# Graph attention layer on one core: where three table merges stand on the vector engine, and the order of the layer norm's steps

## The chip, the cores and the metric

The kernel runs on one core of one Trainium2 chip. The metric is the device time of one execution in microseconds (us). The engines are named as in the profile: PE (TensorE matmul, with its weight loads PEld), DVE (VectorE), ACT (ScalarE), POOL (GpSimd) and SP (SyncE, which issues most DMAs). Each engine works through its own queue in order.

## The reference

`x` is 384 x 1024 (nodes by features). The layer normalises it, projects it to q, k and v, projects each a second time, and runs attention with 16 heads of 64 under a mask built from a list of 6528 typed edges:

```python
h = jnp.maximum(_layernorm(x, axis=-1), 0.0)
q = h @ wq.T + bq;  k = h @ wk.T + bk;  v = h @ wv.T + bv
q2 = (q @ wiq.T + biq).reshape(N, H, D).transpose(1, 0, 2)   # k2, v2 alike
w = jax.nn.softplus(edge_type_weights)
mask = jnp.full((N, N), -jnp.inf).at[src, dst].set(w[edge_type - 1])
mask = mask.at[idx, idx].set(jnp.where(jnp.isneginf(diag), w[3], diag))
scores = jnp.einsum('hnd,hmd->hnm', q2, k2) * scale + mask[None]
out = jnp.einsum('hnm,hmd->hnd', softmax(scores), v2)
return x + (out.transpose(1, 0, 2).reshape(N, OUT_F) @ wo.T + bo)
```

## The kernel before, in words

**Number format.** Matrices are split into a rounded high part and a low part (the remainder). A product is then three matmuls: high x high, high x low and low x high (`mm3`, L367 to L369). Each weight chunk of 128 x 1024 is loaded by SP into `raw` (L65), its high part is made on ACT (`split_hi`, L77) and its low part on DVE or POOL (`split_lo`, L82).

**Layer norm (first part of the span).** The nodes are three tiles of 128. For each tile DVE computes mean and variance (`ln_bn` L251, `ln_mean` L254, with the negated mean on ACT in L257), the mean is subtracted in two halves (`ln_sub`: tiles 0 and 1 on ACT, L280, and POOL, L282; tile 2 on DVE, L284), PE transposes the eight 128 x 128 blocks into two PSUM banks (`ln_transpose`, L292), ACT takes the ReLU as the high part (`ln_hi`, L298) and DVE the low part (`ln_lo`, L303). Division by the standard deviation is postponed: `ln_root` (L260) and `ln_rstd` (L264 to L268) give 1/std per node, `ln_row` (L274, L275) turns it into a row `rrow`, and each projection's result is multiplied by that row (L382, then L383 and L384). `warm(n)` puts n transposes of the identity on PE whose results nobody reads (L309). PE's first real work is the product of weight 0 with the tiles (L414), then weight 1 (L367 to L369).

**Softplus of the edge weights.** `softplus_a` (L157, L158) is on DVE; `softplus_b` (L161, L162, L164: exp, ln, and a small exp) is on ACT and needs it; `softplus_c` (L167, L168) is on DVE again; `mask_values` (L172 to L175) on POOL uses the result.

**The mask.** DVE looks for edges that occur twice (L217), POOL scatters the values into three tables in DRAM (L228), and near the end of the k projections the tables are loaded back (`mask_load`, L237). `mask_select(g)` merges table g into the mask `ma`: one predicated copy of 128 x 1152 on DVE (L241). The first score needs all three.

**Groups of q2 and k2.** Weight chunks 32 to 47 are q2 and k2 of head pairs 0 to 7 in turn: 32 is q2 of pair 0, 33 is k2 of pair 0, 34 is q2 of pair 1, and so on. A group is 24 matmuls into one PSUM bank. Before group w is put on PE, `qk_head(w)` issues the work beside it: `pendq.pop(0)()` is `qk_done` of the group before, which evacuates its bank into `nat` (L377 on ACT, L378 on DVE) and issues the DMAs that stack the parts into `qs` and `ks` (L557 to L567). `split_hi(w + 2)`, `split_lo(w + 2)` and `load(w + 4)` prepare later weights. For the first three groups the order of these steps is a different one (`first`).

**Attention.** One loop goes over 48 steps (16 heads x 3 tiles). It is written out by hand: the scores of step i (`do_S`, L692, two PSUM banks in turn), the softmax steps of earlier i (L698 on DVE reads the scores and adds `ma`; L702 exp on ACT; L706 and L707 normalise), the transposes (L712) and the products with v2 (L729). Between them `fill` puts matmuls of the q2/k2 groups, and later of the output projection. The first 84 units of `fill` (groups 32, 33, 34 and half of 35) come ahead of the first score. The order on each engine is the order of the program; no scheduler changes it.

Of the kernel before, what the change touches and what calls it, by code (L numbers as in the profile page):

```python
# [11 lines left out]
AF = mybir.ActivationFunctionType  # L12
OP = mybir.AluOpType
# [5 lines left out]
EPS = 1e-5  # L19
# [3 lines left out]
def gnn_kernel(ctx: ExitStack, tc: tile.TileContext, x, edges, erows, etw, wq, wk, wv, wiq, wik, wiv, wo,  # L23
# [6 lines left out]
    nc = tc.nc  # L30
# [8 lines left out]
    EB = 8  # L39
    NTAB, RNG = 3, EC // 3  # L40
    JI = [0, 1, 3, 5, 8, 11, 14, RNG]
    WARM = (20, 6, 4)

    def bank(tag):
        return psum.tile([128, 512], F32, tag=tag, name=tag, bufs={"g": 3, "a": 1}.get(tag, 2))
# [14 lines left out]
    def load(w):  # L60
        if w >= NCH:
            return
        n, m = chunks[w]
        raw[w] = wpool.tile([128, D], F32, tag="raw", name="raw", bufs=3)
        nc.sync.dma_start(raw[w], W[n][m])  # L65

    def split_hi(w, dst=None, dve=False):
        if w >= NCH:
            return
        if dst is None:  # L70
            t = wpool.tile([128, 2, D], F32R, tag="whl", name="whl", bufs=4)
            dst = (t[:, 0, :], t[:, 1, :])
        whl[w] = dst
        if dve:
            nc.vector.tensor_copy(dst[0], raw[w])
        else:
            nc.scalar.activation(dst[0], raw[w], AF.Copy)  # L77

    def split_lo(w, eng=None):
        if w < NCH:  # L80
            hi, lo = whl[w]
            (eng or nc.vector).tensor_tensor(lo, raw[w], hi.bitcast(F32), OP.subtract)  # L82

    def split(w, lo_eng=None, dst=None, hi_dve=False):
        split_hi(w, dst, hi_dve)
        split_lo(w, lo_eng)
# [24 lines left out]
    epsc = const.tile([128, 1], F32, name="epsc")  # L111
# [18 lines left out]
    def mask_consts():  # L130
        nc.gpsimd.memset(upper, 1.0)
        nc.gpsimd.affine_select(upper, upper, pattern=[[1, 128]], compare_op=OP.is_gt, fill=0.0, base=0,
                                channel_multiplier=-1)
        nc.gpsimd.iota(dump.bitcast(I32), pattern=[[0, 1]], base=CELLS, channel_multiplier=1)
        nc.gpsimd.tensor_copy(w8[:, 8:9], dump.bitcast(I32))
        nc.gpsimd.memset(zero, 0.0)
# [12 lines left out]
    def mask_floats():  # L149
        nc.gpsimd.tensor_copy(ed.bitcast(F32), ed)  # L150
# [5 lines left out]
    def softplus_a():  # L156
        nc.vector.tensor_scalar(w8[:, 0:4], ew, 0.0, None, op0=OP.max)  # L157
        nc.vector.scalar_tensor_tensor(w8[:, 4:8], ew, -1.0, ew, op0=OP.mult, op1=OP.min)  # L158
# [21 lines left out]
    def key_rows():  # L180

        nc.gpsimd.tensor_copy(kf, er)
        nc.gpsimd.tensor_scalar(kf[:, :EC], kf[:, :EC], float(N), None, op0=OP.mult)
        nc.gpsimd.tensor_tensor(krt[:, :EC], kf[:, :EC], kf[:, EC:], OP.add)
        nc.sync.dma_start(krow.rearrange("c j -> (c j)").rearrange("(p e) -> p e", p=128), krt[:, :EC])
# [53 lines left out]
    def mask_select(g):  # L239

        nc.vector.copy_predicated(ma, mbt[g].bitcast(I32), mbt[g])  # L241
# [4 lines left out]
    var, negm, root, vq, inv, rstd = (lnt[:, c:c + NT] for c in (4, 8, 12, 16, 20, 24))  # L246
    var = lnt[:, 1:2 * NT:2]
    rrow = work.tile([128, 2, N], F32R, tag="qs", name="rrow").bitcast(F32)[:, 0, :]

    def ln_bn(t, h):  # L250
        nc.vector.bn_stats(lnt[:, 30 + 12 * t + 6 * h:36 + 12 * t + 6 * h], xt[t][:, h * 512:(h + 1) * 512])  # L251

    def ln_mean(t):
        nc.vector.bn_aggr(lnt[:, 2 * t:2 * t + 2],  # L254
                          lnt[:, 30 + 12 * t:42 + 12 * t].rearrange("p (a b) -> p a b", a=2))
        if t < 2:
            nc.scalar.mul(negm[:, t:t + 1], lnt[:, 2 * t:2 * t + 1], -1.0)  # L257

    def ln_root():
        nc.scalar.activation(root, var, AF.Sqrt, bias=epsc, scale=0.25)  # L260

    def ln_rstd():

        nc.vector.tensor_scalar(vq, var, 0.25, EPS / 4, op0=OP.mult, op1=OP.add)  # L264
        nc.vector.reciprocal(inv, root)
        nc.vector.tensor_tensor(inv, inv, vq, OP.mult)
        nc.vector.tensor_tensor(root, root, inv, OP.add)
        nc.vector.reciprocal(rstd, root)  # L268
# [8 lines left out]
    def ln_sub(t, c0, c1, eng):  # L277
        src, dst = xt[t][:, c0:c1], xn[t][:, c0:c1]
        if eng is nc.scalar:
            nc.scalar.activation(dst, src, AF.Identity, bias=negm[:, t:t + 1])  # L280
        elif eng is nc.gpsimd:
            nc.gpsimd.tensor_tensor(dst, src, lnt[:, 2 * t:2 * t + 1].to_broadcast([128, c1 - c0]), OP.subtract)  # L282
        else:
            nc.vector.tensor_scalar(dst, src, lnt[:, 2 * t:2 * t + 1], None, op0=OP.subtract)  # L284

    def ln_transpose(t):
        pss = []
        for half in range(2):
            ps = bank("st"[half] if t < 2 else "ga"[half])
            for j in range(4):  # L290
                k = half * 4 + j
                nc.tensor.transpose(ps[:, j * 128:(j + 1) * 128], xn[t][:, k * 128:(k + 1) * 128], ident)  # L292
            pss.append(ps)
        return pss

    def ln_hi(t, half, ps):
        hi = hT[:, 0, half * 4:half * 4 + 4, t * 128:(t + 1) * 128]
        nc.scalar.activation(hi, ps.rearrange("p (k n) -> p k n", k=4), AF.Relu)  # L298

    def ln_lo(t, half, ps):  # L300
        hi = hT[:, 0, half * 4:half * 4 + 4, t * 128:(t + 1) * 128]
        lo = hT[:, 1, half * 4:half * 4 + 4, t * 128:(t + 1) * 128]
        nc.vector.scalar_tensor_tensor(lo, ps.rearrange("p (k n) -> p k n", k=4), 0.0, hi.bitcast(F32),  # L303
                                       op0=OP.max, op1=OP.subtract)

    def warm(n):
        for i in range(n):
            ps = bank("g")
            nc.tensor.transpose(ps[:, :128], ident, ident)  # L309

    mask_consts()
    warm(WARM[0])
    key_rows()
# [5 lines left out]
    ln_mean(0)  # L319
    ln_sub(0, 0, 512, nc.scalar)  # L320
    ln_sub(0, 512, D, nc.gpsimd)
    ln_bn(1, 0)
    ln_bn(1, 1)
    ln_mean(1)
    p0 = ln_transpose(0)
    warm(WARM[1])
    ln_hi(0, 0, p0[0])
    ln_sub(1, 0, 512, nc.scalar)
    ln_sub(1, 512, D, nc.gpsimd)
    ln_bn(2, 0)  # L330
    ln_bn(2, 1)
    ln_mean(2)
    ln_hi(0, 1, p0[1])
    ln_sub(2, 0, 512, nc.vector)
    ln_sub(2, 512, D, nc.vector)
    p1 = ln_transpose(1)
    warm(WARM[2])
    ln_hi(1, 0, p1[0])
# [9 lines left out]
    ln_hi(2, 0, p2[0])  # L348
    ln_hi(2, 1, p2[1])
    ln_root()  # L350
    ln_lo(0, 0, p0[0])
    ln_lo(1, 0, p1[0])
    ln_lo(2, 0, p2[0])
    softplus_a()
    ln_lo(0, 1, p0[1])
    ln_lo(1, 1, p1[1])
    ln_lo(2, 1, p2[1])
    ln_rstd()
    mask_floats()
    split(1, nc.gpsimd)  # L360
    split_hi(2)
# [24 lines left out]
    w = 0  # L386
# [189 lines left out]
    def qk_head(w):  # L576
        first = w - W0 < 3
        if not first:
            load(w + 4)
            split_hi(w + 2)  # L580
        if pendq:
            pendq.pop(0)()
        if first:
            split_hi(w + 2)
        split_lo(w + 2, nc.gpsimd if (w + 2) % 2 == PAR else None)
        if first:
            load(w + 4)
        if 0 < w - W0 <= NTAB:
            mask_select(w - W0 - 1)

    def fill_qk():
        nonlocal w
        for p in range(8):
            for n in ("iq", "ik"):
                tasks.append(lambda w=w: qk_head(w))
                if now[0] < 0:
                    run_tasks()
                gps[w] = bank("g")
                src = qT if n == "iq" else kT
                for k in range(KT):  # L600
                    colmm(gps[w], w, src, k)
                    yield 3
                pendq.append(lambda w=w: qk_done(w))
                w += 1
        tasks.append(lambda: pendq.pop(0)())

    pendq = []
    W0 = 32
# [245 lines left out]
```

## Time and profile before

| what | value |
|---|---|
| median of 3 runs | 305.87 us (305.39 to 306.45) |
| the profiled execution | 305.25 us |
| its span (first to last instruction) | 303.5 us |
| PE busy | 293.2 us, 97% of the span |
| PE clock granted, mean | 0.999 |
| DVE, ACT, POOL busy | 202.3, 154.6, 156.5 us |
| the three merges, L241 | 1.54, 3.75 and 1.44 us, from 151.8, 161.0 and 165.1 us |
| the scores of steps 0, 1, 2 on PE, L692 | from 161.83, 163.22 and 167.35 us |
| first matmul of weight 0, L414 | from 13.22 us |

The span is what the trace covers; the execution's own time is 1.75 us longer. All durations below come from the one profiled execution. A line number such as L241 is a line of the kernel before; a group of instructions is named by line, engine, operation and the tiles that it writes and reads. "us" in a timeline counts from the start of the span.

### The profile page before, as it was taken

The page shows a single profiled execution, that of the slowest core. Times are in us where ns is not written, and L with a number is a line of the kernel's source. Part 1 is how long each engine was busy: PE and PEld are TensorE (multiplying, and loading weights), DVE is VectorE, ACT ScalarE, POOL GpSimd, SP SyncE. Part 2 cuts the span into 40 slices and gives each one's busy share as a digit, 9 for nine tenths or more (in the row PEclk, how much of TensorE's full clock was granted, in tenths as well). Part 3 has the DMA queues.
Part 4 walks back from the last instruction along what each step waited for, and adds up shares of the span by engine and source line. Part 5 has one row for each costly group of instructions (what it writes and reads, how often), then busy time and mean ns, then how long its engine had stood idle before and what let it go on. Part 6 is the DMA issues. An engine that isn't in the chain of part 4 may idle for free.

```text
span 303.5 us, 4966 instructions
## 1 busy us (share of the span) xinstructions
PE 293.2 (97%) x1653; PEld 276.7 (91%) x1653; DVE 202.3 (67%) x493; ACT 154.6 (51%) x288; POOL 156.5 (52%) x164
## 2 busy tenths in 40 slices
PE   6799999999999999999997999999999999999995
PEld 5699999999988889999997999999999998888884
DVE  2968976667756653888629766667675766696523
ACT  3784643334422222555224667767677766676310
POOL 4776676273766785600033547383837466557210
PEclk9999999999999999999999999999999999999999
DMA  7799845645396749393277998556665636910005
GB/s 226 284 293 379 281 148 182 223 144 176 106 311 182 231 147 287 109 350 121 90 183 208 216 209 175 150 150 163 153 171 133 176 108 158 375 57 0 2 0 207
DMA packets 22377, 55.12 MB, mean 182 GB/s; under 512 B 4816, under 2 KB 8400, under 8 KB 22352
## 3 DMA queue, kind: packets, MB, share of 16 engines
q1 hardware_dynamic: 19968, 52.42, 57.0%
q0 software_dynamic: 2064, 1.80, 2.1%
q10 hardware_dynamic: 320, 0.59, 0.9%
q8 instruction: 13, 0.21, 0.3%
q14 instruction: 12, 0.10, 0.1%
HBM read 40.39 MB, written 4.97 MB: 149 GB/s over the span
## 4 chain that ended last, share of the span: by engine, by line
PE 91%; issue 2%; DMA 2%; DVE 2%; ACT 1%; ACTq 1%; SPq 0%; DVEq 0%
PE g L367 20%; PE g L369 20%; PE g L368 20%; PE s L692 6%; PE a L729 6%; PE t L712 5%; DMA g<-in_x_dram 2%; PE s L368 2%; PE s L369 2%; PE s L367 2%; PE t L369 2%; PE t L368 2%; PE t L367 2%; PE g L414 1%; ACTq L567 1%
## 5 line engine op out<-in xcount | busy, mean ns | idle before, releaser
L367 PE MATMUL g<-g,whl 128*128 128x384 f32 x312 | 106.4, 341 | 0.0
L369 PE MATMUL g<-g,whl 128*128 128x384 f32 x312 | 104.5, 335 | 0.0
L368 PE MATMUL g<-g,whl 128*128 128x384 f32 x312 | 104.2, 334 | 0.0
L228 POOL DMA_INDIRECT tab<-val,idx x51 | 57.8, 1133 | 37.4 <-DMA tab<-val,idx 10.8
L77 ACT ACTIVATE whl<-raw 128x1024 fp32r<-128x1024 f32 x51 | 53.4, 1051 | 31.6 <-PE g L369 21.1
L707 POOL TENSOR_TENSOR e<-e,s 128x384 f32<-128x384 f32 x48 | 39.1, 828 | 43.1 <-DVE s L706 34.7
L82 DVE TENSOR_TENSOR whl<-raw,whl 128x1024 fp32r<-128x1024 f32 x41 | 50.2, 1224 | 15.5 <-ACT whl L77 15.5
L368 PEld LDWEIGHTS g<-g,whl 128*128 128x128 f32 x312 | 58.7, 188 | 0.0
L367 PEld LDWEIGHTS g<-g,whl 128*128 128x128 f32 x312 | 58.6, 188 | 0.0
L369 PEld LDWEIGHTS g<-g,whl 128*128 128x128 f32 x312 | 58.5, 188 | 0.0
L82 POOL TENSOR_TENSOR whl<-raw,whl 128x1024 fp32r<-128x1024 f32 x11 | 26.5, 2410 | 37.7 <-ACT whl L77 33.9
L383 ACT ACTIVATE g<-f,bc 128x384 fp32r<-128x384 f32 x24 | 14.8, 618 | 54.5 <-DVE f L382 54.5
L702 ACT ACTIVATE e<-e,s 128x384 f32<-128x384 f32 x48 | 29.4, 612 | 14.7 <-DVE s L698 14.7
L722 DVE TENSOR_TENSOR pt<-t,pt 128x384 fp32r<-128x384 f32 x48 | 26.4, 550 | 14.3 <-ACT pt L721 13.6
L721 ACT ACTIVATE pt<-t 128x384 fp32r<-128x384 f32 x48 | 23.3, 484 | 13.6 <-PE t L712 12.7
L692 PE MATMUL s<-ks,qs 128*128 128x384 f32 x96 | 25.3, 344 | 2.3 <-DVE s L698 2.3
L698 DVE CUSTOM_DVE_ANT_0 e<-s,ma 128x384 f32<-128x384 f32 x48 | 26.3, 550 | 0.9 <-PE s L692 0.5
L382 DVE TENSOR_TENSOR f<-g,rrow 128x384 f32<-128x384 f32 x24 | 13.3, 556 | 15.3 <-PE g L369 15.3
L712 PE MATMUL t<-ident,e 128*128 128x128 f32 x144 | 23.5, 271 | 0.0
L712 PEld LDWEIGHTS t<-ident,e 128*128 128x128 f32 x144 | 18.7, 140 | 3.1
L692 PEld LDWEIGHTS s<-ks,qs 128*128 128x128 f32 x96 | 17.1, 188 | 4.9 <-DVE s L698 4.2
L729 PE MATMUL a<-pt,vhl 128*128 128x384 f32 x96 | 20.8, 351 | 0.0
(147 smaller groups left out, 410.8 us busy)
## 6 DMA issues: line engine op xcount, KB each, us to landing
ks<-nat SPq DMA_DIRECT2D x30, 192.0 KB, 3.5
raw<-in_wv_dram SPq DMA_DIRECT2D x8, 512.0 KB, 5.9
raw<-in_wq_dram SPq DMA_DIRECT2D x8, 512.0 KB, 3.4
raw<-in_wiv_dram SPq DMA_DIRECT2D x8, 512.0 KB, 3.9
raw<-in_wk_dram SPq DMA_DIRECT2D x8, 512.0 KB, 4.6
raw<-in_wiq_dram SPq DMA_DIRECT2D x8, 512.0 KB, 3.7
raw<-in_wik_dram SPq DMA_DIRECT2D x8, 512.0 KB, 4.6
raw<-in_wo_dram SPq DMA_DIRECT2D x8, 512.0 KB, 5.0
```

Source lines behind the costliest of these rows:

```text
L77: nc.scalar.activation(dst[0], raw[w], AF.Copy)
L82: (eng or nc.vector).tensor_tensor(lo, raw[w], hi.bitcast(F32), OP.subtract)
L228: nc.gpsimd.indirect_dma_start(out=tabs[c // RNG], out_offset=bass.IndirectOffsetOnAxis(ap=idx[:, c:c + 1], axis=0), in_=val[:, c:c + 1], ...
L367: nc.tensor.matmul(ps, lhi, rhi, start=first, stop=False)
L368: nc.tensor.matmul(ps, lhi, rlo, start=False, stop=False)
L369: nc.tensor.matmul(ps, llo, rhi, start=False, stop=last)
L692: nc.tensor.matmul(ps[:, :N], qs[:, o, t * 128:(t + 1) * 128], ks[:, o, s, :], start=(s == 0), stop=(s == 1))
L702: nc.scalar.activation(es[i], es[i], AF.Exp, bias=s[:, 0:1], scale=-1.0, accum_out=s[:, 1:2])
L707: nc.gpsimd.tensor_tensor(es[i], es[i], s[:, 2:3].to_broadcast([128, N]), OP.mult)
L712: nc.tensor.transpose(ps[:, k * 128:(k + 1) * 128], es[i][:, k * 128:(k + 1) * 128], ident)
L722: nc.vector.tensor_tensor(lo, pv, hi.bitcast(F32), OP.subtract)
L729: nc.tensor.matmul(ps[:, :N], vhl[:, k, p, 2 * o:2 * o + 2, :], pts[h][:, s, k, :], start=(k == 0 and s == 0), stop=(k == 2 and s == 1))
```

## The change

Merges. The three calls of `mask_select` stand elsewhere: merge 0 at the end of the head of group 32 (before: of 33); merge 1 in the head of group 33, right behind the evacuation of group 32 (before: at the end of the head of 34); merge 2 in the head of group 34, right behind the evacuation of group 33 (before: at the end of the head of 35).

Layer norm. Both ReLUs of tile 0, with the transposes and the 6 filler transposes ahead of them, are issued ahead of the mean of tile 1. The 4 filler transposes between tiles 1 and 2 are gone. The quantity `vq` is computed on ACT behind the square root instead of on DVE in `ln_rstd`. `softplus_a` stands behind `ln_rstd`, that is behind all low parts.

On the engines' queues this is all that differs: no DMA is added, removed or reordered, and POOL's and SP's queues are the same.

```diff
-    WARM = (20, 6, 4)
+    WARM = (20, 6, 0)
...
     def ln_root():
         nc.scalar.activation(root, var, AF.Sqrt, bias=epsc, scale=0.25)
+        nc.scalar.activation(vq, var, AF.Identity, bias=epsc, scale=0.25)
 
     def ln_rstd():
 
-        nc.vector.tensor_scalar(vq, var, 0.25, EPS / 4, op0=OP.mult, op1=OP.add)
         nc.vector.reciprocal(inv, root)
...
     ln_sub(0, 512, D, nc.gpsimd)
+    p0 = ln_transpose(0)
+    warm(WARM[1])
+    ln_hi(0, 0, p0[0])
+    ln_hi(0, 1, p0[1])
     ln_bn(1, 0)
     ln_bn(1, 1)
     ln_mean(1)
-    p0 = ln_transpose(0)
-    warm(WARM[1])
-    ln_hi(0, 0, p0[0])
     ln_sub(1, 0, 512, nc.scalar)
     ln_sub(1, 512, D, nc.gpsimd)
     ln_bn(2, 0)
     ln_bn(2, 1)
     ln_mean(2)
-    ln_hi(0, 1, p0[1])
     ln_sub(2, 0, 512, nc.vector)
...
     ln_lo(2, 0, p2[0])
-    softplus_a()
     ln_lo(0, 1, p0[1])
     ln_lo(1, 1, p1[1])
     ln_lo(2, 1, p2[1])
     ln_rstd()
+    softplus_a()
     mask_floats()
...
         if pendq:
             pendq.pop(0)()
+        if 0 < w - W0 < NTAB:
+            mask_select(w - W0)
         if first:
             split_hi(w + 2)
         split_lo(w + 2, nc.gpsimd if (w + 2) % 2 == PAR else None)
         if first:
             load(w + 4)
-        if 0 < w - W0 <= NTAB:
-            mask_select(w - W0 - 1)
+        if w == W0:
+            mask_select(0)
```

## The prediction

> **What bounds the kernel now.** First the engine row of the page and busy time by stage (columns: stretch, its length, busy us and instructions of PE, PE weight load, DVE, ACT, POOL, granted clock, DMA share, GB/s):
> ```profile
> PE 293.2 (97%) x1653; PEld 276.7 (91%) x1653; DVE 202.3 (67%) x493; ACT 154.6 (51%) x288; POOL 156.5 (52%) x164
> 0.00:18.00 18.00, 13.52 (x81) 12.11 (x82) 11.68 (x26) 10.76 (x18) 12.09 (x24) 1.00 0.76 254
> 18.00:82.00 64.00, 64.00 (x369) 63.65 (x369) 47.29 (x130) 28.09 (x38) 37.71 (x38) 1.00 0.65 217
> 150.00:168.00 18.00, 15.93 (x93) 15.61 (x91) 10.70 (x11) 6.90 (x10) 4.89 (x2) 1.00 0.65 174
> 168.00:262.00 94.00, 94.00 (x568) 90.68 (x568) 62.81 (x189) 67.55 (x159) 55.48 (x53) 1.00 0.68 173
> ```
> TensorE is full between 18 and 150 us and between 168 and 262 us. It has slack only in the layer norm (first 18 us), around 150-168 us, and at the end. So the change can gain only where it closes a TensorE gap, and both its parts sit at one. The waits of PE name them:
> ```profile
> PE s L292 <- ACT g L280: 2.7, 2, 1.7
> PE s L692 <- DVE s L698: 2.3, 2, 2.1
> PE g L414 <- ACT g L298: 0.3, 1, 0.3
> ```
> Second gap: the chain of waits (start us, length us, piece), 159-168 us:
> ```profile
> 159.84 0.04 DVE whl L82
> ...
> 160.99 0.31 DVE ma L241
> 161.30 3.33 issue
> 164.62 0.61 DVE nat L378
> 165.24 1.36 DVE ma L241
> ...
> 166.73 0.15 DVE e L698
> ...
> 167.35 0.62 PE s L692 x2
> ```
> S product 2 (L692) needs the bank that S product 0 gives up at its first read, L698. DVE runs in order, and two table merges (L241), the second and third, stand before that L698. The DVE and POOL timelines give the reason why the second merge is long:
> ```profile
> 160.84 2.50 POOL L82 TENSOR_TENSOR whl<-raw,whl 128x1024 fp32r<-128x1024 f32 x1 [4.19 <-ACT whl L77]
> 160.99 3.75 DVE L241 COPY_PREDICATED ma<-mbs 128x1152 f32<-128x1152 int32 x1
> ```
> POOL ends at 163.34, and 163.34 + 1.44 (the merge of 165.14 took that) is 164.78 against a real end of 164.74. The merge stood still until POOL was done.
>
> First gap: the chain through the layer norm:
> ```profile
> 9.18 0.58 ACT g L298
> 9.76 0.62 ACT g L280
> 10.37 0.04 issue
> 10.42 0.66 PE s L292 x4
> 11.07 0.44 PE t L292 x4
> 11.51 0.49 PE g L309 x4
> 12.01 0.45 PE g L292 x4
> ```
> The ReLU of tile 0 (L298) stands ahead of the subtraction of tile 1 (L280) on ACT, though its input was ready at about 7.6; and four filler transposes (L309) sit between tiles 1 and 2.
>
> [...] The trace agrees: the merge above, and L264 (128x3), which took 1.26 us and ended at 17.21 when POOL's L82 ended (17.19). [...] The trace shows no fall: the longest PE gap here is 1.73 us and the granted clock is 1.00.
>
> **Part A, layer norm.** No DMA moves. Removed: 4 filler transposes on PE and L264 on DVE. Added: one ACT Identity of 128x3; its nearest row is L260, 0.30 us, holding ACT for 0.19 (L260 starts 13.45, the next 13.64). It is in front of the hi split of weight 1.
> 1. ACT. The two ReLUs of tile 0 run when their transposes end (about 7.6 and 8.0), and end near 8.7, before the mean of tile 1 is there (9.03): free. L280 of tile 1 needs its negated mean (L257, 9.07 to 9.27), so it starts at 9.31 as in tile 0 (0.24 after L257) and ends at 10.03, not 10.36. Transposes of tile 1 start at 10.09 against 10.42.
> 2. PE. The second half is loaded by 10.94 (0.85 after, as before; POOL's half, L282, is there at 10.15). Without the filler, tile 2's first half needs only DVE's L284 (first one ends 11.00): about 11.1. Its second half waits for the second L284, 11.75, so it starts at 11.82 and ends at 12.42.
> 3. ACT's ReLU of tile 2: first half starts about 11.76 (0.49 behind the last of tile 1), second at 12.45 against 12.97 before. L414 starts 0.14 after the first of them ends (12.35): 12.5 against 13.22. Its fifth product needs the second ReLU (13.05 + 0.14 = 13.19) and is due at 12.5 + 4 x 0.172 = 13.19. Gain **0.7 us**.
> 4. What is late next: the third product of weight 1 needs POOL's L82. ACT now reaches weight 1 at about 13.31, POOL runs 14.45 to 16.86, and PE wants it at 12.5 + 24 x 0.172 + 0.35 = 16.97. It just fits; I take **0.65**, bounds 0.3 and 0.75. Before, this had 0.5 us to spare, so POOL is the next limit.
> 5. L264 gone: I credit nothing. L266, a DVE product of two SBUF operands, now meets the same POOL L82[...]. The end of L268 moves from 17.89 to about 17.5; PE wants it at 18.7.
> 6. Softplus behind it: its two DVE instructions (0.45 and 0.15[...]) leave the ReLU low parts, which gain 0.45, but Exp on ACT now waits for about 17.9 instead of starting at 16.96. Queued behind it on ACT: two table loads (1.28 each), hi split 3, the row factor L275; behind that on DVE, lo split 3 and the first L382; on POOL, the values (L172). All come about 1 us later. Who waits: weight 3 starts on PE at about 25.5 and needs L382 done (23.3 before, now about 24.0), and the table merges are 125 us away. Cost zero; the cover is 1.5 us.
> 7. Four filler transposes are on the chain for 0.49 us; that is contained in step 2.
>
> **Part B, merges.** Same three instructions, one place earlier each; no DMA moves. They go past these: merge 0 from behind nat of group 32 (q2 of pair 0; groups 33, 34, 35 are k2 0, q2 1, k2 1) to ahead of it; merge 1 from behind lo split 36 to behind nat 32; merge 2 from behind nat 34 to behind nat 33. The DMAs of nat (L557 to L567, on SP and ACT) wait for those L378.
> 1. Merge 0: lo split 34 ends at 149.9, so it runs 149.83 to 151.3; nat 32's L378 was at 151.25. Its qs DMAs slip 0 to 0.1 us; S product 0, which needs the last ks DMA, is set by nat 33. Zero. The tables were issued by 129.84 and landed within 7.1 us, so before 137: no wait.
> 2. Merge 1 takes the place of merge 0: 151.9 to 153.4, POOL idle. Zero.
> 3. Merge 2: behind nat 33, at 155.9, while POOL's L82 runs 154.25 to 156.65: blocked, ends about 158.1. DVE's next work, lo split 36, waits for ACT until 159.84. Zero, with 1.7 us to spare.
> 4. DVE at 161: nat 34 follows ACT (161.22) at 161.25 instead of 164.62, and the first L698 follows S 0 at about 162.4 instead of 166.73. S 2 no longer waits.
> 5. What is late next: the second L698 still stands behind nat 35 and lo split 38. ACT's nat 35 is at 164.81, behind a hi split that waited for a weight load until 163.84; neither moves. So nat 35 165.4, lo split 165.95, second L698 167.1 to 167.65; S 3 at 167.7.
> 6. Sum: from 165.12, where PE stopped, S 2, nine products, S 3 and six products take 0.35 + 1.56 + 0.35 + 1.04 = 3.30, so S 4 was due at 168.42. It came at 171.17: 2.75 lost. After: S 3 due 167.03, comes 167.7: 0.67 lost. Gain **2.1 us**, bounds 1.2 (step 5 a us later, or POOL giving way to merge 2) and 2.75.
> From there PE is full for 94 us and everything is paced by it; the transfers of pair 1 are issued 1.9 us earlier too.
>
> **Sum.** 0.65 + 2.1 = 2.75 us. The profiled execution is 305.25 us (span 303.5 and 1.75 around it): 302.5. The median of the runs, 305.87, is 0.62 above it: **303.1 us**.
>
> **Rivals.**
> - *A new wait takes most of one part* (0.2): S 3 waits a us longer, or weight 1's POOL split eats A. For it: steps A4 and B5 have next to no slack. Against: both were worked out from times that the change leaves alone. Gain 1.3 to 2.0: 303.9 to 304.6.
> - *The gain is given back, or the change does not do what it says* (0.06): PE's later stages wait for DMA. Against: PE is 94.00 of 94 busy, and the pair's DMAs move along. 305.5.
> - *Slower* (0.04): without the four fillers PE's activity from 7 to 13 us falls and the clock drops to half. Half clock costs half of its duration, so it outweighs 2.75 from 5.5 us on[...]: 306.5. Against: the longest gap shrinks from 1.73 to about 1.4 us.
> - *Forecast* (0.7): 303.1, with 302.5 to 303.8 from the bounds and the spread of runs before (305.39 to 306.45).
>
> Range 302.3 to 304.6: it leaves out the two small cases and a little at either edge. A run can tell about 0.3% (0.9 us) from no change: faster 0.9, same 0.06, slower 0.04.
>
> **What would show it.** Right: L414 starts near 12.5; no L241 between 160 and 168, merge 2 over 2 us long around 156; the PE wait for L698 falls from 2.3 to under 1 us and moves to S 3; L266 ends with POOL's L82. Wrong: a PE wait for L82 on POOL near 17 us or for L698 of 2 us, a granted clock under 0.9 in the first 20 us, or a new PE wait in 25-150 us.

## The result, and the profile after

The changed kernel took 302.31 us (median of 6 runs, 301.78 to 302.95), the kernel before 305.63 us in the 6 runs beside it; the ratio is 0.989, 95% interval 0.9863 to 0.9917. Forecast were 303.1 us and 302.3 to 304.6: the sign and the order of size were right, the time lies at the lower end of the range, 0.8 us under the forecast. Against the 305.87 us that the forecast started from, 3.56 us are gone, not 2.75. The two places of the change give about 2.6 of them; where the rest comes from is the main question of the runs below.

The profiled execution took 302.19 us, its span is 300.5 us (303.5 before). Engine row of the page, and busy time by stage (the second stretch is moved 2.7 us against the one shown of before, since all comes earlier; columns as there):

```profile
PE 293.1 (98%) x1649; PEld 276.1 (92%) x1649; DVE 200.5 (67%) x492; ACT 154.9 (52%) x289; POOL 155.7 (52%) x164
0.00:18.00 18.00, 14.46 (x83) 12.55 (x84) 12.11 (x25) 11.05 (x19) 12.15 (x24) 1.00 0.83 254
147.30:165.30 18.00, 18.00 (x106) 18.00 (x105) 11.48 (x13) 7.21 (x11) 4.89 (x2) 1.00 0.70 182
```

PE does the same work (293.1 us), but in the 18 us around the first scores it is now full, where it did 15.93 before; in the first 18 us it does 0.94 us more. The waits of PE:

```profile
PE s L292 <- ACT g L280: 2.0, 2, 1.2
PE s L694 <- DVE s L700: 0.2, 1, 0.2
```

(L694 and L700 are L692 and L698 of before, two lines on.) The wait of 2.3 us for the first read of the scores is down to 0.2, and that of L414 for the ReLU is gone. The merges in the DVE timeline, with the POOL instruction beside the third:

```profile
148.86 1.55 DVE L241 COPY_PREDICATED ma<-mbs 128x1152 f32<-128x1152 int32 x1
150.29 0.61 DVE L378 SCALAR_TENSOR_TENSOR nat<-g,bc,nat 128x384 fp32r<-128x384 f32 x1
150.81 1.55 DVE L241 COPY_PREDICATED ma<-mbs 128x1152 f32<-128x1152 int32 x1
...
154.92 2.43 DVE L241 COPY_PREDICATED ma<-mbs 128x1152 f32<-128x1152 int32 x1
158.71 1.23 DVE L82 TENSOR_TENSOR whl<-raw,whl 128x1024 fp32r<-128x1024 f32 x1 [1.37 <-ACT whl L77]
...
161.39 0.56 DVE L700 CUSTOM_DVE_ANT_0 e<-s,ma 128x384 f32<-128x384 f32 x1 [0.65 <-PE s L694]
```

```profile
153.54 2.40 POOL L82 TENSOR_TENSOR whl<-raw,whl 128x1024 fp32r<-128x1024 f32 x1 [23.13 <-ACT whl L77]
```

The third merge still stands behind POOL (153.54 + 2.40 + 1.44 = 157.38; it ended at 157.35; 1.44 us is what the third merge of before took beside no POOL instruction), but now DVE has nothing to do until 158.71. At 161.39 the first read (L700) waited for the scores, and no longer the scores for the read. The chain through the layer norm:

```profile
7.16 1.30 DVE lnt L251 x2
8.48 0.22 DVE lnt L254
...
8.96 0.73 ACT g L280
9.69 0.04 issue
9.73 0.66 PE s L292 x4
10.39 0.45 PE t L292 x4
10.84 0.01 issue
10.85 0.63 PE g L292 x4
...
11.51 0.66 PE a L292 x4
12.17 0.09 issue
12.26 1.81 PE g L414 x9
```

No ReLU and no filler is on it. But note its start: L251 of tile 1 starts at 7.16 us here and at 7.50 before, because that tile of `x` landed 0.34 us earlier in this execution, which is no work of the change. Counted from there, L414 comes after 5.10 us and not 5.72: 0.62 us gained.

### The profile page after: what moved, and what is told of

It reads as the page before. It is cut to its first block, busy times and chain, and to the rows that moved or that the text cites. A ratio compares the mean times of both kernels' runs of the same rounds, so it can differ in the third digit from the quotient of the medians.

```text
span 300.5 us, 4961 instructions
## 1 busy us (share of the span) xinstructions
PE 293.1 (98%) x1649; PEld 276.1 (92%) x1649; DVE 200.5 (67%) x492; ACT 154.9 (52%) x289; POOL 155.7 (52%) x164
## 4 chain that ended last, share of the span: by engine, by line
PE 95%; DMA 2%; DVE 1%; ACT 0%; issue 0%; SPq 0%
PE g L369 21%; PE g L367 21%; PE g L368 21%; PE s L694 6%; PE a L731 6%; PE t L714 5%; PE s L369 2%; PE s L368 2%; PE s L367 2%; DMA g<-in_x_dram 2%; PE t L369 2%; PE t L367 2%; PE t L368 2%; PE g L414 1%; PE a L369 1%; PE a L367 1%
## 5 line engine op out<-in xcount | busy, mean ns | idle before, releaser
L82 DVE TENSOR_TENSOR whl<-raw,whl 128x1024 fp32r<-128x1024 f32 x41 | 50.2, 1224 | 9.6 <-ACT whl L77 7.9
L82 POOL TENSOR_TENSOR whl<-raw,whl 128x1024 fp32r<-128x1024 f32 x11 | 26.5, 2412 | 35.6 <-ACT whl L77 31.8
L700 DVE CUSTOM_DVE_ANT_0 e<-s,ma 128x384 f32<-128x384 f32 x48 | 26.3, 550 | 2.0 <-PE s L694 1.8
L694 PE MATMUL s<-ks,qs 128*128 128x384 f32 x96 | 25.3, 344 | 0.3 <-DVE s L700 0.2
L378 DVE SCALAR_TENSOR_TENSOR nat<-g,bc,nat 128x384 fp32r<-128x384 f32 x16 | 9.9, 618 | 16.4 <-ACT nat L377 14.4
```

Source lines behind the costliest of these rows:

```text
L694: nc.tensor.matmul(ps[:, :N], qs[:, o, t * 128:(t + 1) * 128], ks[:, o, s, :], start=(s == 0), stop=(s == 1))
```

## The experiments

Each ratio is to the kernel before, run beside it. Two things scatter from run to run: the landing of tile 1 of `x` (its L251 starts at 6.65 to 8.17 us in the profiles), and the granted clock that the records of each run show. In most runs its mean is 0.997 to 1.000, in others about 0.994, in some 0.988. Over all sets of runs beside the experiments the kernel before had 64 of 111 at 0.997 or more, with a median of 305.0 us; 38 near 0.994, 306.4 us; and 9 near 0.988, 307.8 us. "At full clock" below means the runs of the first sort; they are compared with those of before (304.95 us in the first two sets of experiments).

**The two parts alone.** `ln_only` is the change with `mask_select` where it was:

```diff
-        if 0 < w - W0 < NTAB:
-            mask_select(w - W0)
...
-        if w == W0:
-            mask_select(0)
+        if 0 < w - W0 <= NTAB:
+            mask_select(w - W0 - 1)
```

> The layer-norm part alone, merges where they were before. Theory (two independent gaps): the distance from the first statistics of tile 1 (L251) to the first product of weight 0 (L414) falls from 5.72 us to 5.1 us, as in the changed kernel; the S product 2 still waits about 2 us for its bank; time 0.6 to 0.7 us under before (ratio 0.998). Rival (the 0.96 us by which L414 came earlier in the profile of the change is all work of the change): ratio 0.997. Rival (the layer-norm gain is lost again at the second gap, since the weight loads there are not paced by PE): PE wait at S 2 grows by 0.6 us and ratio 1.000.

Measured: ratio 0.9958 (0.994 to 0.9977). At full clock 304.26 us (14 of 22 runs), 0.69 us under before. L251 of tile 1 to L414: 8.13 to 13.23 us, 5.10 us as expected. S 2 still waits:

```profile
PE s L692 <- DVE s L698: 2.1, 2, 1.9
```

So the layer norm gives 0.6 to 0.7 us, and the second gap does not take it back; of the 0.96 us by which L414 came earlier in the profile of the change, 0.34 were landing.

`merges_only` is the kernel before with that edit the other way round.

> The merges moved as in the change, layer norm as before. Theory: PE wait at S 2 gone, 0.2 to 0.7 us left at S 3; 2.1 to 2.4 us under before (ratio 0.992 to 0.993); with the layer-norm part it adds up to the whole change (3.0 to 3.3 us). Rival (the two parts help each other, for instance through transfers that come at another time): less than 1.8 us, sum of the parts under the whole.

Measured: ratio 0.9911 (0.9877 to 0.9946), 303.00 us at full clock (5 of 6 runs), 1.95 us under before, a little less than the 2.1 to 2.4 expected; the wait for the first read of the scores (L700 there) is 0.2 us in its profile. 0.69 + 1.95 = 2.64 us, and the changed kernel at 302.31 is 2.64 us under 304.95. All 19 runs of the changed kernel (given below) have a median of 302.44, which makes it 2.51, so that the agreement to the hundredth is luck. Within the scatter the two parts add up, as two separate gaps should, but to 2.5 to 2.6 us and not to the 3.0 to 3.3 expected for the whole.

**Which merge, and why.** `merge2_left` is the change with merge 2 at the end of the head of group 35:

```diff
-        if 0 < w - W0 < NTAB:
-            mask_select(w - W0)
+        if w - W0 == 1:
+            mask_select(1)
...
-        if w == W0:
-            mask_select(0)
+        if w - W0 in (0, 3):
+            mask_select(0 if w == W0 else 2)
```

> The change, but merge 2 stays at the end of the head of group 35, behind nat 34, as before. Theory (what hurt was merge 1 held up by POOL's low split of weight 37, and with it everything behind it): merge 2 now meets that same POOL instruction, ends with it plus 1.44 us, just after 163 to 164 us; first L698 some 2.5 us later than in the change, S 2 waits 0.2 to 0.6 us, S 3 0.3 to 0.7; 0.3 to 0.6 us over the change, so ratio 0.990 to 0.992 to before. Rival (two merges of 1.44 us each ahead of the first L698 cost their full length): S 2 waits 1.4 us and the time is 1.5 us over the change, ratio 0.994.

```profile
161.00 2.49 POOL L82 TENSOR_TENSOR whl<-raw,whl 128x1024 fp32r<-128x1024 f32 x1 [3.64 <-ACT whl L77]
```

```profile
161.96 2.95 DVE L241 COPY_PREDICATED ma<-mbs 128x1152 f32<-128x1152 int32 x1
...
165.06 0.56 DVE L700 CUSTOM_DVE_ANT_0 e<-s,ma 128x384 f32<-128x384 f32 x1 [0.15 <-DVE ma L241]
```

Those are its POOL and DVE timelines. The merge ends 1.42 us after POOL, as foretold, and the first read comes 2.0 us later against S 0 than in the change. But S 2 follows S 0 after 3.29 us (162.55 to 165.84), exactly as in the change: in this execution it does not wait, where 0.2 to 0.6 us were expected. Ratio 0.9893 (0.9863 to 0.9923); 302.94 us at full clock, 0.5 us over the pooled median of the change. This one profile, a run at 0.994, can't account for that. POOL's split started 1.55 us ahead of S 0 in it; in three profiles of the changed kernel it did so by 1.04, 1.14 and 1.55 us. With 1.14 the first read would end 0.4 us later and S 2 wait about 0.25 us, by my estimate from these figures; no other profile of this kernel is there to show it. The rival's 1.5 us are out. Merge 2 in its old place costs little, then; it was merge 1 beside POOL's split that did the damage.

`lo37_dve` is the kernel before with POOL's instruction taken from beside merge 1:

```diff
-        split_lo(w + 2, nc.gpsimd if (w + 2) % 2 == PAR else None)
+        split_lo(w + 2, nc.gpsimd if (w + 2) % 2 == PAR and w + 2 != 37 else None)
```

> The kernel before, with one edit: the low split of weight 37 goes to DVE instead of POOL, so that no POOL instruction lies beside merge 1. DVE gets 1.22 us more work ahead of the first L698. Theory[...]: merge 1 falls from 3.75 to 1.44-1.55 us, first L698 2.3 - 1.2 = 1.1 us earlier, S 2 waits about 1.0 instead of 2.1 us; time 0.9 to 1.2 us under before (ratio 0.996 to 0.997). Rival (merge 1 is long for another reason, such as waiting for its table): it stays at 3.7 us, and the time is 1.2 us over before (ratio 1.004).

```profile
162.51 1.55 DVE L241 COPY_PREDICATED ma<-mbs 128x1152 f32<-128x1152 int32 x1
```

The merge takes 1.55 us instead of 3.75, with the same table at the same place. S 2 waits 0.9 us instead of 2.1, although DVE now does the split too (some 0.2 us of this is that merge 1 started earlier against S 0, 1.06 us ahead of it and not 0.84); 304.12 us at full clock, 0.83 us under before (all runs: ratio 0.9958, 0.9937 to 0.998). The standstill is POOL's doing, and not the table's; by what mechanism, the runs don't show.

**The clock.** The profile of `lo37_dve` happens to be a run at 0.994, and shows where the clock goes. By stage, and in the PE timeline:

```profile
8.00:10.00 2.00, 0.65 (x6) 0.38 (x4) 1.97 (x5) 0.52 (x2) 0.47 (x1) 1.00 1.02 397
10.00:12.00 2.00, 1.17 (x7) 1.17 (x8) 1.93 (x5) 1.61 (x4) 2.00 (x4) 0.80 0.87 314
12.00:14.00 2.00, 2.00 (x12) 1.94 (x11) 1.37 (x3) 0.85 (x2) 2.00 (x2) 0.50 0.22 54
14.00:16.00 2.00, 1.95 (x11) 1.62 (x10) 1.16 (x4) 1.66 (x4) 0.80 (x2) 0.84 0.99 269
```

```profile
10.83 0.79 PE L292 MATMUL s<-ident,g 128*128 128x128 f32 x4 [2.18 <-ACT g L280]
11.41 1.06 PE L292 MATMUL t<-ident,g 128*128 128x128 f32 x4
12.27 1.06 PE L309 MATMUL g<-ident 128*128 128x128 f32 x4
```

The clock (the third number from the right) is 0.5 for 0.8 + 2 + 0.64 = 3.4 us, if in the slices at either edge it was 1.00 or 0.50 and nothing between: four transposes take 1.06 us where they took 0.60. Before it, PE had rested 2.18 us for a late tile 1, but it was not idle all the time: in the 3.4 us up to the fall at 11.2 us it was busy for 1.22. Runs with one such stretch are 1.4 us longer (306.4 against 305.0 us above); by the forecast's count, half of its duration, it would be 1.7.

In the profiles the length of that rest goes with the fall. The five that show one (this, `merge2_left` and three kernels below, `small_back`, `nat36_pool` and `warm_none`) rested 1.82 to 2.42 us ahead of tile 1's transposes, the nine that rested there without a fall 0.40 to 1.84 us. Counted in the same way, the stretch is 3.4 us long in `merge2_left` and `small_back` too, and 6.8 us in `warm_none`. What ends the rest is the landing of tile 1 (DVE waited for it until 7.91 us in `lo37_dve`, until 7.16 in the change). The length alone does not decide it: in the profile of before, PE rested 2.07 us for L698 and the clock stayed at 1.00. The stretch lies in the layer norm that the change rearranges, so the next four kernels ask whether the change has a part in it. `after_same` is the changed kernel:

> The changed kernel itself, beside the others. Runs so far fall into groups by their mean granted clock: 1.00, and 0.994 with about 1.5 us more. In the kernel before, 21 of 42 runs had 0.994 or less; in the changed kernel none of 6. Theory (a stretch of half clock in the layer norm, which a PE that rests too long there draws; the change shortens the rest): under a quarter of the runs at 0.994, runs at full clock 2.6 us under those of before (304.95, so 302.3), median ratio 0.988 to 0.990. Rival (the frequency is the chip's luck and the same for all kernels): half of the runs at 0.994, median ratio 0.991.

Measured: 302.68 us, none of 7 runs at 0.994; ratio 0.9918 (0.9882 to 0.9953). The other three change `WARM` alone, the number of fillers: `warm_none` is the change with (20, 0, 0), `fill14` the change with (20, 14, 0), `before_fill14` the kernel before with (20, 14, 4).

> The change without the 6 fillers behind tile 0's transposes as well, so PE rests from 7.8 to 9.7 us. Theory of activity: most runs show 0.994 or less, and are 1.5 us longer; those at full clock stay at 302.3. Rival (the fillers do nothing for the clock): the same share of runs at 0.994 as the changed kernel, same median.

Measured: 17 of 22 runs at 0.994 or less, nine of them near 0.988; median 304.52 us, ratio 0.9963 (0.9943 to 0.9983). Taking out six fillers of 0.11 us gives back about 2 us. It was also expected that its runs at full clock would stay at 302.3; its five such runs lie between 302.17 and 304.66 us, which is a miss. A slow stretch that the record doesn't show (last section) may be in some of them; none of the five has a profile, so that stays open.

> The change with 14 fillers behind tile 0's transposes instead of 6; they take 0.11 us each and end before tile 1's subtraction is there, so none is in the way. Theory of activity: no run at 0.994, median 302.2 to 302.4. Rival: the share of runs at 0.994 is that of the changed kernel.

Measured: none of 9 runs at 0.994; 302.76 us, ratio 0.9916 (0.9886 to 0.9946). That is over the 302.2 to 302.4 expected, but in time it is not to be told from the change, which had no such run either.

> The kernel before with 14 fillers instead of 6 behind tile 0's transposes and nothing else changed. Theory of activity: the half of the runs at 0.994 goes, and the median falls by 0.7 us to that of the runs of before at full clock (304.95), ratio 0.997 to 0.998. Rival (luck of the chip): half of the runs stay at 0.994, ratio 1.000.

Measured: 1 of 22 runs at 0.994, against 16 of the 47 of before beside it; ratio 0.9964 (0.9947 to 0.9982), median 304.53 us. Eight fillers that nobody reads give the kernel before as much as the layer-norm part does. Two things are left open here. The median was expected to fall to 304.95; at full clock too its runs have 304.50 us, 0.46 less than those of before beside it. And its profile has transposes at half rate under a recorded clock of 1.00 (last section), so that the 1 in 22 counts only what the record shows.

**The smaller steps of the layer norm.** `warm_four` is the change with `WARM = (20, 6, 4)`.

> The change with the 4 fillers between tile 1 and tile 2 put back. Theory (they stood on the chain of before, but in the new order the transposes of tile 2 wait for the subtraction on DVE anyway): L414 comes at most 0.1 us later counted from L251 of tile 1 (5.1 us in the change, 5.7 before); runs at full clock 302.3 to 302.7, no run at 0.994. Rival (taking out the fillers is most of the layer-norm gain): 5.5 us, 0.4 us over the change.

Measured: 5.38 us from L251 of tile 1 to L414 (7.71 to 13.09), between the theory's 5.2 and the rival's 5.5. PE put the four fillers from 11.21 us on, and tile 2's transposes started 0.3 us later than without. Time 302.72 us, ratio 0.9894 (0.9866 to 0.9921): about half of the 0.62 us hangs on the fillers by the profile, but in the times that can't be seen.

`small_back` is the change with `vq` on DVE and `softplus_a` between the low parts again:

```diff
-        nc.scalar.activation(vq, var, AF.Identity, bias=epsc, scale=0.25)
...
+        nc.vector.tensor_scalar(vq, var, 0.25, EPS / 4, op0=OP.mult, op1=OP.add)
...
     ln_lo(2, 0, p2[0])
+    softplus_a()
...
     ln_rstd()
-    softplus_a()
```

> The change with vq back on DVE and softplus_a back between the low parts, so that of the layer-norm part only the order of the ReLUs and the fillers is left. Theory (these two edits are worth nothing for PE): L414 at 5.1 us after L251 of tile 1, time that of the change at full clock, 302.3 to 302.7; L264 takes over 1 us again, ending with POOL's L82. Rival (they carry part of the gain, because the low parts or the row factor are late on PE without them): PE waits 0.3 us or more behind L414 or for L274, 0.3 to 0.6 us over the change.

Measured: 302.52 us at full clock (6 of 7 runs), ratio 0.9885 (0.9859 to 0.991), and no wait of PE behind L414: the two edits are worth nothing that these runs can tell. Its profile is a run at 0.994, so its distance to L414 says nothing. The DVE stall changes its place, as forecast, from L264 here to L266 in the change (DVE timelines of this kernel and of the change):

```profile
16.76 1.25 DVE L264 TENSOR_SCALAR lnt<-lnt 128x3 f32<-128x3 f32 x1
```

```profile
15.23 1.40 DVE L266 TENSOR_TENSOR lnt<-lnt 128x3 f32<-128x3 f32 x1
```

Both are 128 x 3 and end with POOL's L82: 15.57 + 2.41 = 17.98 and 14.20 + 2.41 = 16.61.

**What is left at S 3.** In `nat36` the head of group 36 takes the evacuation of group 35 first:

```diff
-        first = w - W0 < 3
+        first = w - W0 in (0, 1, 2, 4)
```

> The change, and in the head of group 36 the evacuation of group 35 goes ahead of the hi split of weight 38 and of load 40. Theory (S 3 waits for the second L698, which stands behind nat 35 and low split 38, and both behind the landing of weight 38): nat 35 starts when its bank is ready, the second L698 comes 0.5 to 0.9 us earlier against the landing, S 3 waits 0.1 us or less; 0.1 to 0.5 us under the change at full clock. Rival (the second L698 follows the landing in either order, through low split 38): S 3 waits as before, 0 to 0.8 us by the landing, and the time is that of the change; load 40 comes later, and costs up to 0.3 us.

Measured: S 3 follows S 2 after 1.91 us, which is no wait; in the profile of the change it was 2.05, in `fill14`, where weight 38 landed late, 2.89. But two more profiles of the changed kernel have 1.91 (`after_same`) and 1.94 (`after_third`): with a weight 38 that lands early there is next to nothing to gain. The time was 302.18 us at full clock (4 of 6 runs), ratio 0.9891 (0.9862 to 0.992). `nat36_pool` also gives low split 38 to POOL:

```diff
-        split_lo(w + 2, nc.gpsimd if (w + 2) % 2 == PAR else None)
+        split_lo(w + 2, nc.gpsimd if (w + 2) % 2 == PAR or w + 2 == 38 else None)
```

> The kernel nat36, and the low split of weight 38 on POOL, so that nothing on DVE between the first and the second L698 waits for weight 38. Theory: second L698 right behind nat 35, about 1.5 us earlier than in the change; S 3 never waits for it; 0.2 to 0.6 us under the change at full clock, 301.8 to 302.3. Rival (the wait moves on: POOL is busy with the split for 2.4 us when the first normalisation L709 comes, so the transposes or S 4 wait): PE wait of 0.3 us or more between 165 and 175 us, no gain.

Measured: 1.91 us again, no new wait on PE, 302.23 us at full clock (4 of 6), ratio 0.9883 (0.9854 to 0.9912). Neither profile has the wait, but the times can't be told from the change's.

**Together.** `nat36_fill12` is `nat36` with `WARM = (20, 12, 0)`, and `after_third` the change again.

> The change, with the evacuation of group 35 ahead of hi split 38 (as in nat36) and with 12 fillers behind tile 0 instead of 6. Theory (activity keeps the clock, and the order keeps S 3 from waiting): no run at 0.994 or less, S 3 0.1 us late at most, median 302.0 to 302.3, which is at or under every other kernel here. Rival (6 fillers are enough and the S 3 wait is rare): the median is that of the changed kernel on the same chip, 302.3 to 302.7; with an early landing of tile 1 the 12 fillers cost 0.1 to 0.2 us.

> The changed kernel once more, on the same chip as nat36_fill12. If its layer norm draws the half-clock stretch as often as in the other kernels that have it (14 of 60 runs so far), one or two of 6 to 10 runs lie at 0.994 with 303.5 to 304; if the 0 of 13 of this kernel is real, none does. Median at full clock 302.3 to 302.7, against 304.9 to 305.3 of before.

Measured: 302.54 us (6 runs, none at 0.994), ratio 0.9882 (0.9836 to 0.9928), and 302.45 us (6 runs, none), ratio 0.9895 (0.985 to 0.994). The 302.0 to 302.3 expected of `nat36_fill12` did not come. S 3 does not wait in its profile (1.91 us), but its 12 fillers ran in part at half rate (2.53 us, where 14 took 1.93 in `fill14`), and tile 1's transposes came 2.93 us after L251 and not 2.57. No version here beats the change clear of noise. All 19 runs of the changed kernel itself are at full clock, median 302.44 us.

## Why the prediction was right or wrong

**Layer norm, steps A1 to A4: right.** 0.65 us was forecast for L414, 0.62 measured from the same start and 0.69 in time. The pieces fit too: L280 0.24 us after L257, tile 1's transposes 2.57 us after L251 (forecast 2.59), tile 2's second half 4.35 (4.32). POOL's split of weight 1 just fits, without a wait.

**A5: right.** L266 took L264's place beside POOL's L82 (it took 1.40 us there, L264 1.26 before) and ended with it (16.63 and 16.61 us). **A6: right in the sum, off in the parts.** PE shows no wait for it, but Exp ran at 17.19 us and not 17.9: L268 was done at 17.04 and not 17.5, with a tile 1 that landed 0.34 us earlier, and L157 took 0.14 us and not 0.45. **A7 on the fillers: too much for them alone.** `warm_four` puts them at 0.28 us in the new order, against 0.49 of the old chain; as A7 was contained in step 2, the sum is not touched.

**Merges, B1 to B4: right.** Merge 0 delays nothing, merge 2 meets POOL and nobody waits, the first read comes 0.54 us after S 0 starts. **B5: right in kind, not constant.** S 3 was to lose 0.67 us. The profile of the change shows 0.2, `fill14` 0.8: it goes with the landing of weight 38, whose high part ACT started 1.5 us after the start of S 0 in one and 2.35 in the other. I took the one profile's landing as fixed.

**B6: about right, with a slip in the sum.** 2.1 us were forecast; 2.33 stand in the pair of profiles (S 4 comes 6.85 us after S 0 against 9.18), 1.95 in time for the part alone. The forecast mixed two views: 165.12 comes from the starts in the timeline, 171.17 from the chain of waits, which sets the same S 4 0.16 us later than the timeline does (171.01). In one view before lost 2.59 us there and not 2.75, and the gain forecast would have been 1.9. Nor is the loss a constant of the old order: S 4 came 9.18 us after S 0 in before, 8.99 in `ln_only` and 8.04 in `before_fill14`, where POOL's split beside merge 1 ran earlier against S 0 (from 2.24 us ahead of it, and 0.99 in before).

**The sum's base: the step that failed.** The gain held; the time that it was taken from did not. I added the 0.62 us between the profiled execution and the median of three runs as though this offset belonged to the kernel, and so put the half clock at nothing for the kernel before, on the record of one execution (0.999). Of 111 runs of that kernel 47 show a stretch of half clock. At full clock its median is 305.0 us, so the base of 305.87 was 0.87 us too high. That runs with the stretch were among the three behind 305.87 is not shown, since their clocks are not on record.

From 305.0 the forecast gain of 2.75 leads to 302.25, and the change's 19 runs at full clock give 302.44: there the change is worth 2.56 us, 0.19 under the forecast, and B6's slip is 0.16 of that. So the 0.68 us by which 303.12 lies over 302.44 are 0.87 of base less 0.19 of gain; that the two sizes in the sum come so close is luck too, with parts that scatter by more. Against the median of 305.63 measured beside the change the base is only 0.24 us too high; the rest of the 0.8 us lies in the difference of these medians, 3.3 us instead of 2.75. It fits runs of before with that stretch among the six and none among those of the change, but the clocks of the six are not on record either.

**The rivals.** "Slower" rested on the half clock, and I turned it down with "the trace shows no fall", from one execution with a gap of 1.73 us in the layer norm. The fall exists: the clock records show it in before itself (47 of 111 runs), and `warm_none` shows that fillers taken from this very place bring it out (17 of 22). Its 306.5 was an estimate that no trace had shown; in the runs of before one stretch goes with 1.4 us, and a clock near 0.988 with 2.8 (307.8 us). For the change as made, the sign was the other way: none of its 19 runs had it. That the change draws it less often is not settled, though. The other kernels with its order of the layer norm and its six fillers had it in 14 of 47 runs (`ln_only` 8 of 22), and what sets the difference was not found. The landing of tile 1 is a candidate: L251 of tile 1 started at 6.65 to 7.73 us in three profiles of the change, and at 7.64 to 8.15 in those of the five others; for the runs without a profile it isn't known. The rival with a new wait was right that one comes at S 3 (0.2 us) and wrong in its size, and no new wait of PE for DMA shows.

## What to carry to other kernels

Before adding a gain to a median, ask which runs the median is made of: a profile at full clock and a median over runs of two clocks are not the same kernel's time. A long instruction that is long in one place alone (3.75 us, and 1.54 and 1.44 elsewhere) is read together with its neighbour on the other engine; here moving the merge to a place where DVE has nothing else to do was worth 2 us (1.95 in `merges_only`), and shortening it was not needed. In a stage where PE rests, filler work that ends before the real input comes cost nothing that could be measured here (`fill14`, 302.76 us, beside 302.68 of `after_same`), and was worth as much as the reordering (`before_fill14`, ratio 0.9964, against 0.9958 of `ln_only`); at half rate it took twice as long (0.22 us a filler, and 0.11) and did not always end in time (`nat36_fill12`, 2.93 us and not 2.57). Take fillers off a chain only where others remain in the gap: in the change's order of the layer norm 14 of 66 runs with six fillers there had the stretch, and 17 of 22 with none (`warm_none`).

## What the runs showed of the hardware

Two things were not expected. The clock fell to half (0.50 from 12 to 14 us) behind a rest of PE of 2.18 us, with PE busy for 1.22 of the 3.4 us ahead (`lo37_dve`); in before it stayed at 1.00 behind 2.07 us. And the granted-clock record can miss half rate altogether: in `before_fill14`, whose mean is 1.00, it shows 1.00 while four transposes take 1.11 us, against 0.66 in before (stage and PE timeline):

```profile
6.00:8.00 2.00, 1.17 (x6) 1.17 (x7) 0.00 (x0) 0.75 (x2) 0.91 (x1) 1.00 0.89 354
```

```profile
6.83 1.11 PE L292 MATMUL s<-ident,g 128*128 128x128 f32 x4 [0.88 <-ACT g L280]
```

This is not a fall but a slow start that goes on. In the profile of before, too, the 20 fillers at the head of the span ran at half rate, 0.22 us each against 0.11 later, under a recorded clock of 1.00:

```profile
1.43 4.46 PE L309 MATMUL g<-ident 128*128 128x128 f32 x20 [1.43 <-POOL ident masks.py:199]
```

There the rate had doubled before the first transposes at 6.88 us (0.66 us for four); in `before_fill14` and `nat36_fill12` (1.11 us each) it doubled only among the fillers behind them. Why then, the runs don't show. So "at full clock" above is the record's word, and the durations of like instructions are the better witness.
